# First unit's gate sums between its projections, and the second half's layernorm and gate products among the first three units

## The chip, the cores and the metric

The kernel runs on one core of one Trainium2 chip. The time is the device time of one execution in microseconds (us). The kernel before took 1453.18 us as the median of three runs (1452.86 to 1455.38). One more execution was profiled; all durations and start times in this document come from such profiled executions, counted from the start of the span.

The engines are PE (TensorE, matrix products), DVE (VectorE), ACT (ScalarE), POOL (GpSimd) and SP (SyncE, which here only issues DMAs). Each works off its own queue strictly in the order in which its instructions were written.

## The reference

The input x is 4 sequences of 256 tokens of 256 features, in float32, 1024 tokens in all. The reference has two stages with a residual each:

```
x = x + layernorm(attention(layernorm(x)))
x = x + layernorm(moe(layernorm(x)))
```

The attention is a gated delta net with 16 query/key heads and 32 value heads of width 128. Two projections feed it. One gives q, k, v and z; q, k and v go through a causal convolution over 4 tokens and a silu. The other, with W_ba, gives two numbers per token and value head, b and a, of which the gates are made:

```
beta = sigmoid(b)
g    = -exp(A_log) * softplus(a + dt_bias)
```

g is summed along each chunk of 64 tokens, and differences of the sums, exponentiated, are the decays that weigh the products k k^T and q k^T of a chunk. A triangular system per chunk is solved, and a recurrent state carries from chunk to chunk. The result is normed, gated with silu(z) and projected back with W_out. The second stage routes each token to 6 of 32 experts, beside 2 shared ones.

## The kernel before, in words

The tokens are cut into two halves of 512. A unit is one query/key head on one half, with its two value heads, so there are 32 units: units 0 to 15 on the first half, 16 to 31 on the second. After the units come the experts for both halves.

**The order is written out by hand.** Every stage is a generator that yields places, numbers on one common axis. A heap (L1009 to L1013) always continues the stage with the lowest place, and the instructions that it issues are appended to the queues of PE, ACT, DVE and POOL. So a place decides nothing but the order in the queues. `at(turn, slot)` is turn * 9 + slot; unit u begins at `at(u, 0)` and is spread over about six turns, so several units are in work at any time. `places(p, s)` gives p, p + s, p + 2s and so on. SP's queue is not written by hand: the framework orders the DMAs by itself, from when it thinks that each can go.

**entry(h)** (L207) makes half h ready: it loads x (`load_x`, tile xn), does the layernorm (L188 and L189 statistics on DVE, four times; L190 on DVE and L191, a pow, on POOL; L194 normalises on DVE, four times), transposes it to xT (L204 on PE, L205 copies on ACT), and multiplies with W_ba (L220 on PE, tile pba). Then come the gate sums: the sigmoid to beta (L230, ACT), a + dt_bias (L233, DVE), Abs and Exp (L240, L241, ACT), two sums (L246, L247, DVE), a logarithm (L249, ACT), and reciprocal, products and sums (L250 to L255, DVE). Then the products: cumulative sums of g on PE (L260, L263, tile pc), copied on ACT (L267), negated into ng on DVE (L269, L270), transposed on PE (L278, tile pg), copied on ACT (L279) and stored to DRAM as g_rows (L280). The first group of steps has the places `first`, the products have `second`.

**The stages of a unit.** `weights` loads the projections' weights (L296 w, L303 wz, L307 wo). `decays` loads gw, the unit's rows of g_rows on all partitions (L321), and makes decays of it: POOL adds a mask (L327), and either ACT takes Exp with a bias (unit 0, L338, eight of them) or POOL adds ng (L346) and ACT takes two wide Exps (L350). `prepare` projects q, k and two v (L390, tiles pj_0 to pj_3, PE), convolves (L398 on ACT, three L400 on DVE for each), takes the silu of two at a time (L410, ACT), transposes k and q (L419, ptn_1 and ptn_0) and sums the squares (L421, ACT), makes kk, its reciprocal and br (L427 to L431, DVE) and nk (L435, POOL), multiplies k with k and q (L442 and L461, tiles pk) and weighs the products with the decays (L446 and L464, DVE, tile am). Part of am goes to DRAM as mb (L480). v is transposed and scaled to vp (L490, L493). `blocks`, once for two units, loads small diagonal blocks (L507 wm, L513 on ACT), inverts them on DVE (L514 to L550, tiles quad, dd, prod), stores them (L555 db) and loads them as diag (L563, eight DMAs). `solve` has POOL make e of am (L587), and PE multiplies diag with e (L579, py) and goes on from there. `gate` projects z (L364, pz). `finish` makes the outputs (L664 to L704), transposes them (L736, copied by ACT in L737 to hT) and projects them (L742, pp).

**small** (L772) brings the router's weights and the experts' biases b1 into the chip; b1 is turned by two trips through PE (L791, L800) and DRAM (L794 to L797). It uses the tile `temp`, of which there is one, as do the gate sums. The tile xn, for x, exists once as well.

PSUM tiles under the tag "ms" (pt_a, pba, pc, pg, ptn, pk, ptv, pz) share two banks; the projections pj have two banks of their own. A PE instruction waits until the bank it writes has been read by whoever reads it.

Of the kernel before, what the change touches and what calls it, by code (L numbers as in the profile page):

```python
# [9 lines left out]
AF = mybir.ActivationFunctionType  # L10
# [53 lines left out]
def gated_delta_net_moe(  # L64
# [139 lines left out]
                nc.tensor.transpose(pt[:, i, :], src[:, i, k * P : (k + 1) * P], ident)  # L204
            nc.scalar.copy(xT[:, k, h * T : (h + 1) * T], pt.rearrange("p a b -> p (a b)"))  # L205

    def entry(h, first, second):  # L207

        tl = slice(h * NL, (h + 1) * NL)
        yield next(first)  # L210
        if h:
            load_x("a", h)
        xn = xns[h]
        yield from layernorm(first, xn, xn, 1e-5, f"a_{h}")
        yield from transposed(first, xn, h, f"a_{h}")
        yield next(first)
        pba = bank("ms", [P, NL, HQK, 2, R], f"pba_{h}")
        for t in range(NL):
            for k in range(2):
                nc.tensor.matmul(  # L220
                    pba[:, t].rearrange("p a b c -> p (a b c)"),
                    xT[:, k, h * T + t * P : h * T + (t + 1) * P],
                    wba[:, k, :],
                    start=(k == 0),
                    stop=(k == 1),
                )
        temp = u1.tile([P, 13, NL * HV // 2], F32, tag="temp", name=f"temp_{h}")
        u, sp, w, lw, g = (temp[:, 2 * i : 2 * i + 2, :].rearrange("p a (t h) -> p (a t) h", h=HV) for i in range(5))
        gs = temp[:, 10:13, :].rearrange("p x (b h) -> p b x h", h=HV)
        nc.scalar.activation(  # L230
            beta[:, tl].rearrange("p t (a c) -> p t a c", c=R), pba[:, :, :, 0, :], AF.Sigmoid
        )
        nc.vector.tensor_tensor(  # L233
            u.rearrange("p t (a c) -> p t a c", c=R),
            pba[:, :, :, 1, :],
            dtb.rearrange("p (a c) -> p a c", c=R).unsqueeze(1).to_broadcast([P, NL, HQK, R]),
            ALU.add,
        )
        yield next(first)
        nc.scalar.activation(sp, u, AF.Abs)  # L240
        nc.scalar.activation(sp, sp, AF.Exp, scale=-1.0)  # L241
        if h == 0:
            nc.scalar.activation(alg, alg, AF.Exp)
        yield next(first)

        nc.vector.tensor_scalar(w, sp, 1.0, None, ALU.add)  # L246
        nc.vector.scalar_tensor_tensor(sp, w, 1.0, sp, ALU.subtract, ALU.subtract)  # L247
        yield next(first)
        nc.scalar.activation(lw, w, AF.Ln)  # L249
        nc.vector.reciprocal(w, w)  # L250
        nc.vector.tensor_tensor(sp, sp, w, ALU.mult)
        yield next(first)
        nc.vector.tensor_tensor(sp, lw, sp, ALU.subtract)
        nc.vector.scalar_tensor_tensor(sp, u, 0.0, sp, ALU.max, ALU.add)
        nc.vector.scalar_tensor_tensor(  # L255
            g, sp, -1.0, alg.unsqueeze(1).to_broadcast([P, NL, HV]), ALU.mult, ALU.mult
        )
        yield next(second)
        pc = bank("ms", [P, 3, 2, HV], f"pc_{h}")
        nc.tensor.matmul(  # L260
            pc[:, :2].rearrange("p a b h -> p (a b h)"), inc, g.rearrange("p t h -> p (t h)"), start=True, stop=True
        )
        nc.tensor.matmul(  # L263
            pc[:, 2], ones, g.rearrange("p (b x) h -> p b x h", x=2)[:, :, 0, :], start=True, stop=True
        )
        pcb = pc[:, :2].rearrange("p a b h -> p (a b) h").rearrange("p (b x) h -> p b x h", x=2)
        nc.scalar.copy(gs[:, :, 0:3:2, :], pcb)  # L267
        yield next(second)
        nc.vector.tensor_tensor(gs[:, :, 1, :], pc[:, 2], gs[:, :, 2, :], ALU.add)  # L269
        nc.vector.tensor_scalar(  # L270
            ng[:, tl].rearrange("p (b x) h -> p b x h", x=2), gs[:, :, 0:3:2, :], -1.0, None, ALU.mult
        )
        gr = u1.tile([NE, 2 * 3 * P], F32, tag="gr", name=f"gr_{h}")
        for b in range(2):
            yield next(second)
            pg = bank("ms", [HV, 3, P], f"pg_{h}_{b}")
            for x in range(3):
                nc.tensor.transpose(pg[:, x, :], gs[:, b, x, :], ident)  # L278
            nc.scalar.copy(gr[:HV, b * 3 * P : (b + 1) * 3 * P], pg.rearrange("p a b -> p (a b)"))  # L279
        nc.sync.dma_start(g_rows[:, h * 6 * P : (h + 1) * 6 * P], gr[:HV])  # L280
# [9 lines left out]
    def weights(u):  # L290

        hq = units[u][0]
        c = hq * 6 * P
        yield at(-1, 3)
        w = wp.tile([P, 2, 4 * P], F32, tag="w", name=f"w_{u}")
        nc.sync.dma_start(w, w_qkvz[:, c : c + 4 * P].rearrange("(k p) o -> p k o", p=P))  # L296
        state[u]["w"] = w
        if u == 0:
            nc.sync.dma_start(cw, conv_w)
            nc.sync.dma_start(nw, norm_w)  # L300
        yield at(2, 4)
        w = wp.tile([P, 2, 2 * P], F32, tag="wz", name=f"wz_{u}")
        nc.sync.dma_start(w, w_qkvz[:, c + 4 * P : c + 6 * P].rearrange("(k p) o -> p k o", p=P))  # L303
        state[u]["wz"] = w
        yield at(4, 1)
        w = wp.tile([P, R, D], F32, tag="wo", name=f"wo_{u}")
        nc.sync.dma_start(  # L307
            w, w_out[hq * R * P : (hq + 1) * R * P, :].rearrange("(r p) d -> p r d", p=P)
        )
        state[u]["wo"] = w  # L310
        yield at(4, 5)
        nc.gpsimd.tensor_scalar(w, w, nw, None, ALU.mult)

    def decays(u):

        hq, bp = units[u]
        yield at(-1, 6) if u > 1 else 7.3 - at(u, 0)
        gw = u2.tile([P, R, 2, 3, P], F32, tag="gw", name=f"gw_{u}")
        state[u]["gw"] = gw
        with tc.issue_after(state[u - 2]["wm"].ins) if u > 2 and u % 2 else nullcontext():  # L320
            state[u]["gw_load"] = nc.sync.dma_start(  # L321
                gw.rearrange("p r b x c -> p r (b x c)"),
                g_rows[hq * R : (hq + 1) * R, bp * 6 * P : (bp + 1) * 6 * P].partition_broadcast(P),
            )
        yield at(0, 1.5) if u else 7.5
        gd = gw.rearrange("p r b x c -> p (r b) x c")[:, :, 0:3:2, :]
        nc.gpsimd.tensor_tensor(  # L327
            gd, gd, neg.unsqueeze(1).unsqueeze(1).to_broadcast([P, 2 * R, 2, P]), ALU.add
        )
        if u == 0:  # L330
            for b in range(2):
                for r in range(R):
                    yield 10.4 + 0.4 * b + 0.2 * r
                    h = hq * R + r
                    for x in range(2):
                        t = bp * NL + 2 * b + x
                        y = gw[:, r, b, 2 * x : 2, :] if x == 0 else gw[:, r, b, 2:3, :]
                        nc.scalar.activation(y, y, AF.Exp, bias=ng[:, t, h : h + 1])  # L338
            return

        for x, cols in enumerate((slice(0, 2), slice(2, 3))):
            for r in range(R):
                n = cols.stop - cols.start
                g = ng[:, bp * NL + x : (bp + 1) * NL : 2, hq * R + r]
                y = gw[:, r, :, cols, :].rearrange("p b x c -> p b (x c)")
                nc.gpsimd.tensor_tensor(y, y, g.unsqueeze(2).to_broadcast([P, 2, n * P]), ALU.add)  # L346
        for r in range(R):
            yield at(0, 4.2) + 0.8 * r
            y = gw[:, r].rearrange("p b x c -> p (b x c)")
            nc.scalar.activation(y, y, AF.Exp)  # L350
# [420 lines left out]

    def small():  # L772

        yield at(3, 0)
        full = nh // P
        raw = u1.tile([P, 13, NL * HV // 2], F32, tag="temp", name="b1_raw")
        flat_, turned = raw[:NE, 2:5, :].rearrange("p a b -> p (a b)")[:, :DH], raw[: full + 1, 6:8, :]
        turned = turned.rearrange("p a b -> p (a b)")[:, :P]
        b1f = dram.tile([nh], F32, name="b1f")
        cuts = (slice(0, P), slice(P, DH))  # L780
        with tc.issue_after(state[1]["wm"].ins):
            nc.sync.dma_start(rw, router_w.rearrange("(k p) e -> p k e", p=P))
            nc.sync.dma_start(rb, router_b.partition_broadcast(P))
            nc.sync.dma_start(b2s, b2)
            for i, rows in enumerate(cuts):
                nc.sync.dma_start(raw[: rows.stop - rows.start, i, :NE], b1[rows, :])
        yield at(4, 0.65)
        pb = bank("ms", [NE, DH], "pb1")
        for i, rows in enumerate(cuts):
            n = rows.stop - rows.start  # L790
# [1 line left out]
        nc.scalar.copy(flat_, pb)  # L792
        nc.vector.memset(turned, 0.0)
        nc.sync.dma_start(b1f.rearrange("(e h) -> e h", h=DH), flat_)  # L794
        yield at(4, 0.66)
        nc.sync.dma_start(turned[:full], b1f[: full * P].rearrange("(i p) -> i p", p=P))
        nc.sync.dma_start(turned[full:, : nh - full * P], b1f[full * P :].rearrange("(i p) -> i p", i=1))  # L797
        yield at(5, 0.65)
        pb = bank("ms", [P, full + 1], "pb1t")
        nc.tensor.transpose(pb, turned, ident[: full + 1, : full + 1])  # L800
        nc.scalar.copy(b1s, pb)
# [185 lines left out]
    def begin(place, stage):  # L987
        heapq.heappush(parts, (place + next(stage), len(begun), place, stage))
        begun.append(stage)

    stages = [
        entry(0, places(-9, 0.3), places(6.8, 0.1)),
        entry(1, places(at(6, 0), 1.4), places(at(12, 0), 1.4)),
        small(),
        zeros(),
        post(0, places(at(HQK + 4, 6), 1.4)),
# [66 lines left out]
```

## Time and profile before

| | |
|---|---|
| median of three runs | 1453.18 us (1452.86 to 1455.38) |
| the profiled execution | 1453.36 us |
| its span | 1451.6 us |
| PE busy | 1373.8 us, 95% of the span |
| weight loads of PE busy | 917.4 us, 63% |
| ACT busy | 854.8 us, 59% |
| DVE busy | 833.8 us, 57% |
| POOL busy | 554.0 us, 38% |

The profile's page gives busy times, the span in 40 slices with a digit for the busy tenths of each, and groups of instructions. A timeline lists instructions in order of time: start, duration, engine, source line, operation, output and inputs, count, and in brackets the idle time of the engine just before it and what ended it. For a group of several instructions the duration is that from the first start to the last end. Starts on PE overlap, since matrix products are pipelined. One product in float32 is recorded as two rows, so a projection pj is four. "SPq" is the issue of a DMA, not its transfer. "PEclk" is the share of its full clock that PE was granted.

### The profile page before, as it was taken

To read this page: it belongs to the slowest core of one execution; us is meant where nothing else is said; L and a number is where in the kernel's file an instruction comes from. 1 tells how busy PE (TensorE), PEld (TensorE's weight loads), DVE (VectorE), ACT (ScalarE), POOL (GpSimd) and SP (SyncE) were. 2 spreads that over 40 slices of the span, in tenths; PEclk is the share of its full clock that TensorE was granted. 3 is DMA by queue.
4 is the path that set the end of the run, shared out by engine and by line. 5 is a ranking of instruction groups with operands and counts; after the bars stand their busy time and mean duration, and the time that the engine had idled before them with its cause. 6 is when DMAs were issued, how large, how long until landed. Compare 5 with 4: busy or idle time off the path is not lost.

```text
span 1451.6 us, 29732 instructions
## 1 busy us (share of the span) xinstructions
PE 1373.8 (95%) x11655; PEld 917.4 (63%) x11655; DVE 833.8 (57%) x1726; ACT 854.8 (59%) x2086; POOL 554.0 (38%) x430
## 2 busy tenths in 40 slices
PE   5669999999999999999999999999899999999996
PEld 3336777777777777777777677777765544444443
DVE  4576685867576686758768686766522243232122
ACT  3657768777777777777777777777443222222121
POOL 1354454555454455545544555545511100000000
PEclk9779999999999999999999999999999999999998
DMA  3443433425242442524243342523333565555531
GB/s 117 119 105 90 96 80 93 98 66 128 59 119 70 96 95 65 127 76 105 71 110 72 88 99 74 133 65 81 78 102 91 142 159 140 149 155 149 154 84 35
DMA packets 310156, 146.40 MB, mean 101 GB/s; under 512 B 240780, under 2 KB 281150, under 8 KB 310018
## 3 DMA queue, kind: packets, MB, share of 16 engines
q1 hardware_dynamic: 310018, 144.51, 39.5%
q8 instruction: 93, 1.52, 0.4%
q14 instruction: 45, 0.37, 0.1%
HBM read 129.40 MB, written 15.06 MB: 100 GB/s over the span
## 4 chain that ended last, share of the span: by engine, by line
PE 77%; ACT 11%; DVE 7%; issue 3%; DMA 2%; POOL 1%; POOLq 0%; SPq 0%; ACTq 0%; DVEq 0%
PE ph L915 11%; PE py L935 11%; PE pj L390 9%; PE pz L364 7%; PE pp L742 7%; PE py L579 4%; PE pu L664 4%; PE po L679 4%; PE pd L579 4%; ACT junk L421 3%; DVE c L400 3%; ACT junko L688 3%; PE pk L461 2%; PE pm L711 2%; PE pk L442 2%
## 5 line engine op out<-in xcount | busy, mean ns | idle before, releaser
L400 DVE SCALAR_TENSOR_TENSOR c<-pj,cw,c 128x510 f32<-128x510 f32 (+2 forms) x384 | 286.3, 746 | 153.2 <-ACT c L398 144.1
L702 POOL TENSOR_TENSOR rs<-rs,nhalf 128x4 f32<-128x4 f32 x64 | 66.6, 1040 | 505.0 <-DVE rs L698 295.2
L390 PE MATMUL pj<-xT,w 128*128 128x512 f32 x512 | 247.4, 607 | 4.7 <-DVE c L400 4.6
L918 ACT ACTIVATE h<-ph,b1s 128x512 f32<-128x512 f32 (+1 forms) x94 | 64.6, 687 | 242.6 <-PE ph L915 242.4
L915 PE MATMUL ph<-xT,we 128*128 128x512 f32 (+1 forms) x376 | 177.4, 594 | 2.0 <-ACT phi L615 1.3
L935 PE MATMUL py<-hg,we 128*128 128x512 f32 (+1 forms) x376 | 176.4, 593 | 0.0
L924 DVE TENSOR_TENSOR hg<-h,gb 128x512 f32<-128x512 f32 (+1 forms) x94 | 65.8, 701 | 186.4 <-ACT h L918 180.5
L398 ACT ACTIVATE c<-pj,cw 128x512 f32<-128x512 f32 x128 | 87.4, 685 | 139.3 <-PE pj L390 138.8
L587 POOL TENSOR_TENSOR e<-am,cst 64x1024 f32<-64x1024 f32 x64 | 151.5, 2367 | 2.4
L390 PEld LDWEIGHTS pj<-xT,w 128*128 128x128 f32 x512 | 95.1, 196 | 77.6 <-issue 73.4
L742 PE MATMUL pp<-wo,hT 128*128 128x256 f32 x512 | 126.0, 389 | 7.7 <-ACT hT L737 5.3
L935 PEld LDWEIGHTS py<-hg,we 128*128 128x128 f32 (+1 forms) x376 | 71.3, 190 | 90.5 <-issue 89.1
L742 PEld LDWEIGHTS pp<-wo,hT 128*128 128x128 f32 x512 | 95.8, 192 | 45.4 <-ACT hT L737 31.1
L694 DVE TENSOR_TENSOR hm<-po,sz 128x512 f32<-128x512 f32 x64 | 43.8, 685 | 135.1 <-ACT junko L688 123.2
L364 PE MATMUL pz<-wz,xT 128*128 128x256 f32 x512 | 121.2, 380 | 0.0
L915 PEld LDWEIGHTS ph<-xT,we 128*128 128x128 f32 (+1 forms) x376 | 69.6, 189 | 80.9 <-issue 78.1
L346 POOL TENSOR_TENSOR gw<-gw,ng 128x512 f32<-128x512 f32 (+1 forms) x124 | 99.3, 832 | 2.4
L364 PEld LDWEIGHTS pz<-wz,xT 128*128 128x128 f32 x512 | 92.5, 190 | 10.4 <-issue 0.5
L191 POOL TENSOR_TENSOR rs_d<-rs_d,nhalf 128x2 f32<-128x2 f32 x4 | 2.8, 696 | 248.0 <-DVE rs_d L190 248.0
L446 DVE SCALAR_TENSOR_TENSOR am<-pk,br,gw 128x512 f32<-128x512 f32 x128 | 89.9, 744 | 6.4 <-ACT gw L338 4.5
L442 PE MATMUL pk<-c 128*128 128x512 f32 x128 | 74.3, 663 | 17.3 <-DVE am L446 10.2
L327 POOL TENSOR_TENSOR gw<-gw,cst 128x1024 f32<-128x1024 f32 x32 | 75.4, 2357 | 35.4 <-DMA gw<-g_rows 35.4
(183 smaller groups left out, 2704.1 us busy)
## 6 DMA issues: line engine op xcount, KB each, us to landing
gw<-g_rows SPq DMA_DIRECT2D x32, 768.0 KB, 6.5
w<-in_w_qkvz SPq DMA_DIRECT2D x32, 512.0 KB, 4.0
diag<-db SPq DMA_DIRECT2D x128, 128.0 KB, 3.2
we<-in_w SPq DMA_DIRECT2D x126, 128.0 KB, 2.9
gb<-gate_rows SPq DMA_DIRECT2D x34, 256.0 KB, 3.8
wz<-in_w_qkvz SPq DMA_DIRECT2D x32, 256.0 KB, 2.7
wo<-in_w_out SPq DMA_DIRECT2D x32, 256.0 KB, 2.7
mb<-am SPq DMA_DIRECT2D x64, 128.0 KB, 2.7
```

The lines of the kernel that those rows point to most:

```text
L346: nc.gpsimd.tensor_tensor(y, y, g.unsqueeze(2).to_broadcast([P, 2, n * P]), ALU.add)
L364: nc.tensor.matmul(pz[:, j].rearrange("p r e -> p (r e)"), xT[:, k, t * P : (t + 1) * P], state[u]["wz"][:, k, :], start=(k == 0), stop=(k ...
L390: nc.tensor.matmul(pj.rearrange("p b s -> p (b s)"), state[u]["w"][:, k, col * P : (col + 1) * P], xT[:, k, bp * T : (bp + 1) * T], start= ...
L398: nc.scalar.activation(y, pj, AF.Copy, scale=cw[:, row, 3:4])
L400: nc.vector.scalar_tensor_tensor(y[:, :, back:], pj[:, :, : S - back], cw[:, row, 3 - back : 4 - back], y[:, :, back:], ALU.mult, ALU.add,)
L442: nc.tensor.matmul(pk, s[:, 1, b * S : b * S + P], s[:, 0:2, b * S : (b + 1) * S], start=True, stop=True)
L446: nc.vector.scalar_tensor_tensor(am[:, r, b, 0:4, :].rearrange("p (i x) c -> p i (x c)", i=2), pk, br[:, 2 * b, r : r + 1], gw[:, r, b, 0: ...
L579: nc.tensor.matmul(po[to, h, :], lhsT[g, h, :], rhs[g, h, :], start=True, stop=True)
L587: nc.gpsimd.tensor_tensor(e[g], mt[g, :, g].unsqueeze(1).to_broadcast(full), lev[g].unsqueeze(2).to_broadcast(full), ALU.mult,)
L742: nc.tensor.matmul(pp[:, b, :], hT[:, b, r, :], state[u]["wo"][:, r, :], start=(r == 0), stop=(r == R - 1))
L915: nc.tensor.matmul(ph[:rows], w[:, k * P : k * P + rows], xT[:, k, c], start=(k == 0), stop=(k == 1))
L935: nc.tensor.matmul(py[m], w[:rows, 2 * P + m * P : 2 * P + (m + 1) * P], hgs[i // 3][:rows, i % 3 * T : (i % 3 + 1) * T], start=False, sto ...
```

## The change

The gate sums and the second half's preparation get other places, and two operations move:

- In `entry`, the places are split in three: `first` for layernorm, transposes and the product with W_ba, a new `middle` for the rest of the gate sums, `second` for the products. For the first half, `middle` runs before unit 0's projections as before, and the products go from place 6.8 to 4.65, between its second and third projection. For the second half, `first` starts at 19.0 in steps of 0.6 (turn 2) instead of 54 in steps of 1.4; `middle` starts at 54, and the products stay at 108.
- The Exp of A_log goes to the beginning. The sigmoid is taken last, after the logarithm; until then beta holds a plain copy of b.
- Unit 0's gw is taken at place 4.7 and its mask added at 4.8; the tile of unit 1's wz is taken a turn earlier.
- `small` goes from turns 3 to 5 to turns 14 to 16, behind the last use of `temp` by the second half's gates.

```diff
-    def entry(h, first, second):
+    def entry(h, first, middle, second):
         tl = slice(h * NL, (h + 1) * NL)
         yield next(first)
         if h:
             load_x("a", h)
+        else:
+            nc.scalar.activation(alg, alg, AF.Exp)
...
-        nc.scalar.activation(
-            beta[:, tl].rearrange("p t (a c) -> p t a c", c=R), pba[:, :, :, 0, :], AF.Sigmoid
-        )
+        nc.scalar.copy(beta[:, tl].rearrange("p t (a c) -> p t a c", c=R), pba[:, :, :, 0, :])
...
-        yield next(first)
+        yield next(middle)
         nc.scalar.activation(sp, u, AF.Abs)
         nc.scalar.activation(sp, sp, AF.Exp, scale=-1.0)
-        if h == 0:
-            nc.scalar.activation(alg, alg, AF.Exp)
-        yield next(first)
+        yield next(middle)
         nc.vector.tensor_scalar(w, sp, 1.0, None, ALU.add)
         nc.vector.scalar_tensor_tensor(sp, w, 1.0, sp, ALU.subtract, ALU.subtract)
-        yield next(first)
+        yield next(middle)
         nc.scalar.activation(lw, w, AF.Ln)
         nc.vector.reciprocal(w, w)
         nc.vector.tensor_tensor(sp, sp, w, ALU.mult)
-        yield next(first)
+        nc.scalar.activation(beta[:, tl], beta[:, tl], AF.Sigmoid)
+        yield next(middle)
...
     def weights(u):
-        yield at(2, 4)
+        yield at(2, 4) - (at(1, 0) if u == 1 else 0)
...
     def decays(u):
-        yield at(-1, 6) if u > 1 else 7.3 - at(u, 0)
+        yield at(-1, 6) if u > 1 else (4.7, 7.3 - at(1, 0))[u]
...
-        yield at(0, 1.5) if u else 7.5
+        yield at(0, 1.5) if u else 4.8
...
     def small():
-        yield at(3, 0)
+        yield at(14, 0)
...
-        with tc.issue_after(state[1]["wm"].ins):
+        with tc.issue_after(state[11]["wm"].ins):
...
-        yield at(4, 0.65)
+        yield at(15, 0.65)
...
-        yield at(4, 0.66)
+        yield at(15, 0.66)
...
-        yield at(5, 0.65)
+        yield at(16, 0.65)
...
-        entry(0, places(-9, 0.3), places(6.8, 0.1)),
-        entry(1, places(at(6, 0), 1.4), places(at(12, 0), 1.4)),
+        entry(0, places(-9, 0.3), places(-3, 0.3), places(4.65, 0.01)),
+        entry(1, places(19.0, 0.6), places(at(6, 0), 1.4), places(at(12, 0), 1.4)),
```

What it does to the queues, read from the built program: on PE, pc and pg stand before pj_2 of unit 0; the second half's pt_a_0 stands before pj_3 of unit 2, and pt_a_1 and pba behind it. On DVE, the second half's statistics stand between br, am and L400 of turn 2, the first L194 before L464 of unit 1, the next ones around L400 of pj_2 of unit 2, and L233 among the quads. On POOL, L191 stands behind the e of unit 0. On ACT, Abs and Exp stand before the squares at the beginning of turn 6, and logarithm and sigmoid after the copy of that turn's second projection. On SP, w of unit 2 stands behind gw and db instead of before g_rows, the loads of `small` leave the place before the first db<-dd, and b1f and its two loads stand among eight loads of diag.

## The prediction

> **What bounds the kernel now.** I read the page's slices first.
>
> ```profile
> PE   5669999999999999999999999999899999999996
> ...
> DVE  4576685867576686758768686766522243232122
> ...
> POOL 1354454555454455545544555545511100000000
> PEclk9779999999999999999999999999999999999998
> ```
>
> Each digit is a slice of 36.3 us. From the fourth slice on PE is full and its clock is granted whole; only the first three (5, 6, 6 tenths) hold idle PE. So a change can do two things: move the moment at which PE becomes full, or change PE's work and its short waits after it. I call the first the entry. Then the timelines of the engines, to see what the entry waits for:
>
> ```profile
> 97.56 0.45 PE L579 MATMUL py<-diag,e 64*64 64x64 f32 x2 [5.58 <-DMA diag<-db]
> ```
>
> ```profile
> 35.43 0.35 SPq L280 DMA_DIRECT2D g_rows<-gr  x1
> 37.28 0.89 SPq L321 DMA_DIRECT2D gw<-g_rows  x2
> ...
> 90.02 1.29 SPq L555 DMA_DIRECT2D db<-dd  x2
> 93.14 6.03 SPq L563 DMA_DIRECT2D diag<-db  x8
> ```
>
> ```profile
> 68.28 0.16 DVE L427 TENSOR_SCALAR kk<-ss 128x4 f32<-128x4 f32 x1
> ...
> 73.92 1.65 DVE L464 SCALAR_TENSOR_TENSOR am<-pk,br,gw 128x256 f32<-128x256 f32 x4
> 76.54 2.31 DVE L400 SCALAR_TENSOR_TENSOR c<-pj,cw,c 128x510 f32<-128x510 f32 x3 [0.97 <-ACT c L398]
> 79.31 2.31 DVE L400 SCALAR_TENSOR_TENSOR c<-pj,cw,c 128x510 f32<-128x510 f32 x3 [0.45 <-ACT c L398]
> ...
> 83.47 0.15 DVE L523 TENSOR_TENSOR quad<-dd 128x8 f32<-128x8 f32 x1 [1.77 <-issue]
> ```
>
> The entry is at 97.56: PE's first solve product waits 5.58 us for diag, which follows db<-dd at 90.02, which follows DVE's chain from quad at 83.47. Before that DVE and ACT take turns, and the whole row hangs on gw, loaded after g_rows at 35.43. I call "shift" how much later (plus) or earlier (minus) an instruction stands than in the row of before.
>
> **Step 1, gate sums (L230 to L255), start of the span.** The sigmoid goes behind the logarithm, the Exp of alg goes to the front (its input must be in by 10.37, when ACT first copies). Gone from the path are the load at L241 (16.11 to 17.40, 1.29) and alg's place in the queue (17.62 to 17.85, 0.23): DVE's first L400 moves from 21.66 to 20.14, -1.52. The sigmoid's load and itself (1.28 + 0.28) now stand after Ln on ACT, 17.84 to 19.4; the copy of the first projection follows (0.59, to 20.0) just under DVE's 20.14, so the cover is 0.14 and whatever ACT is later than that goes onto the path. The row has the Exp 1.29 after the start of its load, with nothing between. [...]
>
> **Step 2, the products between projections two and three.** Six L400 end at 24.66. The silu's load and silu (26.25 to 28.61 before) end at 27.07, the copy of pc (0.26) at 27.33; from L269 to the store took 1.77 (33.66 to 35.43), so g_rows goes out at 29.1, shift -6.3. w_2 no longer stands before it on SP: its load waits until pj_3 of unit 0 is done (33.9) and is wanted at 54.5, so it is covered. gw lands 8.3 after the store (35.43 to 43.69) at 37.4, POOL's L327 (2.35) ends at 39.8.
>
> The price: pj_2 and pj_3 of unit 0 stand behind pg on PE, so they start at 28.56 instead of 24.11. From 24.11 to the copy of pj_3 took 5.36 at half clock, so that copy is at 33.9, DVE's two triples (2.22 each) end at 37.25 (33.74 before), the silu's end starts the squares at 38.26 and the next projection's copy at 39.7. Then the Exp's load (1.29) and eight Exps (46.13 to 48.91, 2.78): c pj_1 of unit 1 starts at 44.35, 48.91 before. pk_2 and am follow at -4.4, and the mb store of unit 0 goes from 54.88 to 50.5. **Shift after the first unit -4.4.** It could be -6.3, all of g_rows' lead, or -3.2, what the first am pair has (43.4 against 46.67); I take the value of ACT's queue, since it releases what follows.
>
> **Step 3, the second half's layernorm in turn 2.** kk of unit 1 is at 63.9. DVE now carries four bn pairs among am and L400 (about 0.53 each): the last ends at 71.6. Next on DVE stands the first of four normalisations (L194), waiting for POOL's pow (L191), and behind it L464 of unit 1, L400 of pj_2 and pj_3, qe, the quads. POOL's queue has the pow behind e:
>
> ```profile
> 68.52 1.02 POOL L435 TENSOR_TENSOR nk<-kk,half 128x4 f32<-128x4 f32 x1 [15.86 <-DVE kk L427]
> 69.51 2.35 POOL L327 TENSOR_TENSOR gw<-gw,cst 128x1024 f32<-128x1024 f32 x1
> 71.94 3.19 POOL L346 TENSOR_TENSOR gw<-gw,ng 128x512 f32<-128x512 f32 x4
> 75.08 4.81 POOL L587 TENSOR_TENSOR e<-am,cst 64x1024 f32<-64x1024 f32 x2
> ```
>
> nk starts with kk, so at shift -4.4 e ends at 75.5 and the pow (1.04) at 76.55: DVE stands still 4.9. Then L194 (0.34), L464 (1.55) to 78.5, L194, L400, two L194, to 81.8. On PE the transposes pt_a_0 stand before pj_3 of unit 2 and need all four normalisations: pj_3 starts at 81.95 instead of running ahead. PE was nearly idle from 72.6, and its clock will be at half:
>
> ```profile
> 72.39 3.29 PE L390 MATMUL pj<-xT,w 128*128 128x512 f32 x4
> ...
> 76.39 1.88 PE L390 MATMUL pj<-xT,w 128*128 128x512 f32 x4
> ```
>
> The first of these rows is a projection at half clock (next start 3.13 later), the second one at full clock (1.72). I take 3.13, the row after a like idle; the other end is 1.4 less. The copy is at 85.25, DVE's triple runs 85.95 to 88.2 (79.31 to 81.5 before). pt_a_1 and its copy (0.58) end at 86.45, pba takes 1.9 (1.74 + 0.17 in its row at 230.51; 3.25 in the first, at 11.86: the upper end is 1.4 more), its copy ends at 88.65, and L233, put between the quads, takes 0.29. The second quad stands at 89.0 against 83.85: **entry shift +5.15**. In terms: -4.4, bn 2.2, POOL wait 4.9, normalisations 1.4, wait for pj_3 4.15, L233 0.1, minus DVE's own waits in that stretch that vanish (0.97 + 0.45 + 1.77 = 3.2). Ends: +1.9 (shift -6.3, full clock) and +7.8 (shift -3.2, slow pba).
>
> **Step 4, work taken out of the full stretch.** Turn 7 loses the transposes (0.53 at 220.08, 0.44 at 226.56) and pba (1.74): -2.7 of PE.
>
> **Step 5, waits in the full stretch.** Between 200 and 280 PE waited 0.32, 0.81 (behind a bn on DVE), 1.72 (for hT, behind the loads at L241 and L410) and 1.14 (for the squares): 4.0, of which 3.4 go; stretches without this work have 0.1 to 0.2 in 40 us. Now Abs, load and Exp (1.83) stand before the squares of turn 6:
>
> ```profile
> 180.45 0.58 ACT L737 COPY hT<-pth 128x512 f32<-128x512 f32 x1
> ```
>
> pp starts on PE at 181.09, when that copy has just ended (181.03): +1.6. Load, Ln, load, sigmoid (3.1) stand before the squares of ptn_0: pk_2 waits 1.0 more, so 2.6 in all. Net -0.8; ends -3.4 (all hidden) and +1.5 (the full 4.9 felt).
>
> **Step 6, the b1 preparation, turns 3 to 5 to turns 14 to 16.** PE, ACT and DVE pieces cost the same there. SP gets the store b1f and two loads among the eight diag loads. The fourth diag load stands at +1.3 (three issues at 0.45 each, the landing of b1f, 1.5, mostly under two diag issues); in the steady rows it lands at 480.0 for a product at 480.55: +0.8, ends 0 and 2. The five small loads leave SP at 81.87 to 84.1, where it was idle. xn_b moves ahead of db<-dd, ready when pt_a_1 is done (86), 9 us before db<-dd at 95.2. The places of gw and wz change no order on POOL, and wz_1 was issued at 5.69 already: 0.
>
> **Sum.** +5.15 - 2.7 - 0.8 + 0.8 = +2.45. The profiled execution took 1453.36 (span 1451.6 and 1.76 around it); it becomes 1455.8. The median of the runs is 0.18 lower: **1455.6**.
>
> **Rivals.**
> - Slower still: the burst of table loads in turn 6 is felt in full (+1.5 for -0.8), b1f holds diag for 2 and pba runs at 3.25. 2.45 + 2.3 + 1.2 + 1.4 = +7.3, 1460.5. For it: ACT had no slack at 180.45. Against it: the squares of ptn_0 release only pk_2.
> - Faster: DVE does not stand behind e. Place: POOL's queue in turn 2; price 4.9, and 1.4 more as PE then keeps its clock: 2.45 - 6.3 = -3.9, 1449.3. It decides once the wait for the pow with what follows falls by 5.4. Against it: e runs directly behind L346 in the row of before, and the pow is queued behind it.
> - The loss is given back: the turn 6 loads and b1f hide under PE's own work; 5.15 - 2.7 - 3.4 = -0.95, 1452.2. For it: ACT is idle 3.8 us before its next projection copy at 184.84. Against it: PE is in order and has hardly any slack to take from.
>
> **How the numbers follow.** What this kernel's runs can tell from no change is about 0.2%, 2.9 us. My forecast has 0.45, with its own range 1453.6 to 1457.8, of which some two fifths lies beyond 2.9; slower still 0.27; faster 0.13; given back 0.15. So slower 0.19 + 0.27 = 0.46, same 0.26 + 0.15 = 0.41, faster 0.13. The range leaves out most of the faster case and the top of the slowest: 1450.3 to 1461.0.
>
> **What would show it.** g_rows' store near 29 and the first mb store near 50.5 (steps 1, 2); a DVE wait of about 5 us on POOL before L194 near 71 to 76, with e just before the pow (step 3); py at about 102.7 for 97.56; PE waits near turn 6 and none around 250 (step 5); one late diag near turn 15 (step 6). The forecast is wrong if DVE's wait is short, if the entry is not near +5, or if the later PE waits are not within 2 us of those named.

## The result, and the profile after

The changed kernel took 1461.56 us (median of 7 runs, 1457.51 to 1463.65); the kernel before, in the same comparison, 1455.42 (7 runs, 1452.86 to 1458.23). The ratio is 1.0036, with a 95% interval of 1.002 to 1.0052: 5.2 us slower. (The two medians alone lie 6.1 apart; this document goes by the ratios throughout.) The profiled execution took 1461.47, its span is 1459.6 against 1451.6.

The page's slices:

```profile
PE   5759989999999999999999999999899999999997
...
DVE  4666767768576676868777586767522143131222
...
POOL 1433545456554545655554455545421100000000
PEclk9879999999999999999999999999999999999998
```

PE has more to do in the second slice (7 for 6) and less in the third and the sixth (5 for 6, 8 for 9): the third slice, 73 to 109 us, holds the later entry, the sixth, 182 to 219, turn 6. SP's timeline, the issues of the DMAs:

```profile
29.39 0.35 SPq L279 DMA_DIRECT2D g_rows<-gr  x1
31.21 0.89 SPq L321 DMA_DIRECT2D gw<-g_rows  x2
...
50.26 1.36 SPq L480 DMA_DIRECT2D mb<-am  x2
...
95.14 1.35 SPq L555 DMA_DIRECT2D db<-dd  x2
98.21 6.07 SPq L563 DMA_DIRECT2D diag<-db  x8
```

g_rows goes out 6.04 earlier (35.43 before), mb of unit 0 4.62 earlier (54.88), db<-dd 5.12 later (90.02). What lies between the last two is POOL's and DVE's turn 2, here from the timelines of these engines:

```profile
67.05 3.19 POOL L346 TENSOR_TENSOR gw<-gw,ng 128x512 f32<-128x512 f32 x4
70.20 4.77 POOL L587 TENSOR_TENSOR e<-am,cst 64x1024 f32<-64x1024 f32 x2
75.05 1.02 POOL L191 TENSOR_TENSOR rs_a<-rs_a,nhalf 128x4 f32<-128x4 f32 x1
```

```profile
71.04 1.53 DVE L190 TENSOR_SCALAR rs_a<-mv_a 128x4 f32<-128x4 f32 x1
76.11 0.41 DVE L194 TENSOR_SCALAR xn_a<-xn_a,mv_a,rs_a 128x256 f32<-128x256 f32 x1 [3.53 <-POOL rs_a L191]
76.43 1.66 DVE L464 SCALAR_TENSOR_TENSOR am<-pk,br,gw 128x256 f32<-128x256 f32 x4
...
85.98 2.31 DVE L400 SCALAR_TENSOR_TENSOR c<-pj,cw,c 128x510 f32<-128x510 f32 x3 [4.71 <-ACT c L398]
...
88.97 0.16 DVE L523 TENSOR_TENSOR quad<-dd 128x8 f32<-128x8 f32 x1
```

The pow stands behind e, and DVE behind the pow: from 71.04, when the sum L190 could start, to 76.11 there is no other work on DVE. Then it stands 4.71 for the copy of pj_3, which PE could not begin before all four normalisations. On PE, ptv_1 of unit 1 stands ahead of both the transposes and pj_3, and waits for L464, which is behind the pow too:

```profile
78.14 1.11 PE L490 MATMUL ptv<-cst,c 128*128 128x128 f32 x4 [5.63 <-DVE am L464]
79.05 0.63 PE L204 MATMUL pt_a<-cst,xn_a 128*128 128x128 f32 x2
81.00 0.80 PE L204 MATMUL pt_a<-cst,xn_a 128*128 128x128 f32 x2 [1.32 <-DVE xn_a L194]
81.59 3.62 PE L390 MATMUL pj<-xT,w 128*128 128x512 f32 x4
```

The entry, on PE's timeline:

```profile
102.55 0.44 PE L579 MATMUL py<-diag,e 64*64 64x64 f32 x2 [6.02 <-DMA diag<-db]
```

It is 4.99 later than before. Had the rest gone as predicted, the kernel would have gained 2.7 after it; it lost 3 instead. Where, is best seen in the shift of one mark per turn, the first product of pz_0 (L364), which stands in turn u + 3 for unit u. Each number is the start in the kernel's own PE timeline minus that of before (107.86, 134.25, 167.86, 199.96, 235.30, 269.65 for units 0 to 5). Unit 3's mark lies behind the beginning of turn 6, where the gate sums now are; "again" is a second profile of the changed kernel, and the others are the experiments below.

| kernel | unit 0 | 1 | 2 | 3 | 4 | 5 | 11 | 15 |
|---|---|---|---|---|---|---|---|---|
| changed | 6.38 | 5.93 | 9.02 | 13.51 | 11.30 | 8.51 | 8.53 | 9.05 |
| changed, again | 5.33 | 4.88 | 5.07 | 8.94 | 6.23 | 3.43 | 3.42 | 3.70 |
| first unit's part alone | -4.83 | -4.82 | -5.75 | -5.76 | -5.76 | -4.12 | -4.13 | -4.12 |
| second half's part alone | 10.44 | 9.99 | 10.37 | 14.23 | 11.49 | 8.70 | 8.70 | 8.98 |
| pow before e | 3.19 | 4.12 | 4.83 | 11.06 | 8.45 | 5.65 | 5.65 | 5.94 |
| transposes behind pj_3 | 7.09 | 8.01 | 10.30 | 14.19 | 11.52 | 8.73 | 8.72 | 9.00 |
| late gate sums | 8.42 | 7.97 | 11.50 | 10.96 | 7.17 | 7.17 | 8.57 | 8.85 |
| normalisations early | -3.34 | -3.80 | -3.20 | 0.66 | -2.10 | -4.90 | -4.93 | -4.66 |
| layernorm in gaps | -1.31 | -1.77 | 1.18 | 0.63 | -3.15 | -3.15 | -2.05 | -1.77 |
| all in gaps | 0.54 | 0.09 | -0.77 | -1.31 | -5.10 | -7.89 | -7.90 | -7.62 |
| all in gaps, tight | -3.59 | -2.69 | -1.58 | -2.13 | -5.91 | -8.71 | -8.73 | -8.47 |

The changed kernel loses at the entry, in turn 5 (unit 1 to 2, +3.09) and in turn 6 (unit 2 to 3, +4.49), and gains 5.0 in turns 7 and 8. Turn 6 on PE's timeline:

```profile
191.75 3.57 PE L742 MATMUL pp<-wo,hT 128*128 128x256 f32 x8 [1.75 <-ACT hT L737]
...
202.51 1.13 PE L461 MATMUL pk<-c 128*128 128x256 f32 x4 [2.20 <-ACT junk L421]
```

The eight products of pp take 3.57 where 1.99 is usual. The busy times in stretches of 2 us (PE, PEld, DVE, ACT, POOL, then PE's granted clock, the DMA share and GB/s) tell why: the clock fell to half just as pp began.

```profile
190.00:192.00 2.00, 0.25 (x1) 0.26 (x2) 0.75 (x1) 1.66 (x6) 0.00 (x0) 0.89 0.00 0
192.00:194.00 2.00, 2.00 (x5) 1.58 (x6) 1.86 (x6) 0.00 (x0) 0.29 (x1) 0.50 0.00 0
194.00:196.00 2.00, 2.00 (x6) 1.28 (x5) 1.91 (x6) 0.00 (x0) 1.92 (x3) 0.76 0.00 0
```

### The profile page after: what moved, and what is told of

Same layout as the page of the kernel before. It is cut to its first block, busy times and chain, and to the rows that moved or that the text cites. A ratio compares the mean times of both kernels' runs of the same rounds, so it can differ in the third digit from the quotient of the medians.

```text
span 1459.6 us, 29731 instructions
## 1 busy us (share of the span) xinstructions
PE 1376.9 (94%) x11655; PEld 919.6 (63%) x11655; DVE 837.1 (57%) x1726; ACT 853.9 (59%) x2086; POOL 553.8 (38%) x430
## 3 DMA queue, kind: packets, MB, share of 16 engines
q8 instruction: 93, 1.52, 0.4%
## 4 chain that ended last, share of the span: by engine, by line
PE 77%; ACT 10%; DVE 7%; DMA 3%; issue 2%; POOL 1%; SPq 0%; POOLq 0%; ACTq 0%; DVEq 0%
PE ph L915 11%; PE py L935 11%; PE pj L390 10%; PE pz L364 7%; PE pp L742 7%; PE py L579 4%; PE pu L664 4%; PE po L679 4%; PE pd L579 4%; ACT junk L421 3%; DVE c L400 3%; ACT junko L688 2%; PE pm L711 2%; PE pk L461 2%; PE pk L442 2%
## 5 line engine op out<-in xcount | busy, mean ns | idle before, releaser
L400 DVE SCALAR_TENSOR_TENSOR c<-pj,cw,c 128x510 f32<-128x510 f32 (+2 forms) x384 | 286.2, 746 | 157.0 <-ACT c L398 147.9
L364 PE MATMUL pz<-wz,xT 128*128 128x256 f32 x512 | 121.2, 380 | 0.0
L346 POOL TENSOR_TENSOR gw<-gw,ng 128x512 f32<-128x512 f32 (+1 forms) x124 | 99.3, 832 | 2.4
L364 PEld LDWEIGHTS pz<-wz,xT 128*128 128x128 f32 x512 | 92.5, 190 | 10.4 <-issue 0.5
L191 POOL TENSOR_TENSOR rs_d<-rs_d,nhalf 128x2 f32<-128x2 f32 x4 | 2.8, 696 | 248.0 <-DVE rs_d L190 248.0
L688 ACT ACTIVATE junko<-po 128x128 f32<-128x128 f32 x256 | 71.1, 278 | 29.2 <-PE po L683 12.0
```

Of the source, the lines that this page charges most:

```text
L364: nc.tensor.matmul(pz[:, j].rearrange("p r e -> p (r e)"), xT[:, k, t * P : (t + 1) * P], state[u]["wz"][:, k, :], start=(k == 0), stop=(k ...
L400: nc.vector.scalar_tensor_tensor(y[:, :, back:], pj[:, :, : S - back], cw[:, row, 3 - back : 4 - back], y[:, :, back:], ALU.mult, ALU.add,)
L688: nc.scalar.activation(junk, po[:, b, r, :], AF.Square, accum_out=os_[:, x, b, r : r + 1])
```

## The experiments

My theory was: the first unit's part is a gain of 4.4, the second half's layernorm costs 9.5 in the ramp because DVE stands behind POOL's queue and PE behind DVE, and the table loads of turn 6 give back part of what turns 7 and 8 gain. The rivals were that the two parts do not add, that the ramp's loss has another cause than the queues, and that turn 6 lost its time otherwise than by the gate sums.

**First unit's part alone.** `first` of the second half, its gate sums and `small` stand where they were.

```diff
-        entry(1, places(19.0, 0.6), places(at(6, 0), 1.4), places(at(12, 0), 1.4)),
+        entry(1, places(at(6, 0), 1.4), places(at(6, 0) + 16.8, 1.4), places(at(12, 0), 1.4)),
...
-        yield at(14, 0)
+        yield at(3, 0)
```

> The first unit's part alone: the gate sums and products between its second and third projection, sigmoid last; the second half's layernorm, gate sums and the b1 preparation where the kernel before has them. Theory (the first unit's part is a gain of 4.4 at the entry, and the loss is all the second half's): py's first product at 93.2 instead of 97.56, time 1451.0, ratio 0.9970 (0.996 to 0.998). Rival (an earlier entry is swallowed by later waits in turns 3 to 8, for diag and on ACT, as the changed kernel lost 3.1 in turn 5): py at 93.2 but ratio 0.9985 or more.

Measured: 1449.41, ratio 0.9966 (0.9952 to 0.9979). PE's timeline (this kernel's lines lie six further down, L585 is L579):

```profile
92.80 0.45 PE L585 MATMUL py<-diag,e 64*64 64x64 f32 x2 [5.50 <-DMA diag<-db]
```

The entry is 4.76 earlier, and nearly all of it is kept. The theory holds; the rival falls.

**Second half's part alone.** The first unit as in the kernel before, everything else as in the changed one.

```diff
-        entry(0, places(-9, 0.3), places(-3, 0.3), places(4.65, 0.01)),
+        entry(0, places(-9, 0.3), places(-9 + 3.6, 0.3), places(6.8, 0.1)),
```

> The second half's part alone: its layernorm in turn 2, its gate sums in turn 6 with the sigmoid last, the b1 preparation in turns 14 to 16; the first unit as in the kernel before. Theory (the two parts add): py's first product at 97.56 + 4.99 + 4.4 = 106.95, time 1455.4 + 5.2 + 4.4 = 1465, ratio 1.0066 (1.005 to 1.008). Rival (without the lead of the first unit the pow's wait hides under waits that DVE and PE have in the ramp anyway): py at 104 or earlier, ratio 1.0045 or less.

Measured: 1463.12, ratio 1.0069 (1.0052 to 1.0085). Here too L585 is L579.

```profile
107.24 0.45 PE L585 MATMUL py<-diag,e 64*64 64x64 f32 x2 [6.08 <-DMA diag<-db]
```

The entry is 9.68 later than before; -4.76 and +9.68 make 4.92, against 4.99 in the changed kernel. The parts add, at the entry and in the ratios (-0.0034 and +0.0069 against +0.0036).

**Pow before e.** The fourth bn pair and, with it, L190 and the pow have in the changed kernel the same place as e, 21.4, and e goes first. Here they have 21.39.

```diff
-        entry(1, places(19.0, 0.6), ...
+        entry(1, itertools.chain((19.0, 19.6, 20.2, 20.8, 21.39), places(22.001, 0.6)), ...
```

> The changed kernel, with the fourth bn pair of the second half's layernorm one hundredth of a slot earlier (place 21.39 for 21.40), so that its pow (L191) stands in POOL's queue just before e of unit 0 instead of just behind it; on DVE the fourth bn pair and L190 come before the am pair of pk_1 instead of after it; nothing else moves. Theory (POOL's queue makes DVE stand): the stand of DVE before the first L194 falls from about 4.9 us to 1.0 to 1.5, py's first product comes at 98 to 99 instead of 102.55, the time falls by about 4, to 1457.5, ratio to the kernel before 1.0010 (1.000 to 1.002). e ends about 1 to 2 us later, which nobody waits for. Rival (the layernorm's own DVE work and pt_a_0 standing before pj_3 set the entry, and the wait for the pow only took time in which DVE would have stood anyway): py at 101.5 or later, time within 1 of the changed kernel, ratio 1.003 or more.

Measured: 1458.53, ratio 1.0026 (1.0012 to 1.0041), py at 99.88: 2.7 to 3.1 earlier than in the two profiles of the changed kernel (102.55 and 102.96), not 4. POOL and DVE:

```profile
70.32 1.02 POOL L191 TENSOR_TENSOR rs_a<-rs_a,nhalf 128x4 f32<-128x4 f32 x1
71.31 4.77 POOL L587 TENSOR_TENSOR e<-am,cst 64x1024 f32<-64x1024 f32 x2
```

```profile
71.48 2.33 DVE L194 TENSOR_SCALAR xn_a<-xn_a,mv_a,rs_a 128x256 f32<-128x256 f32 x1
73.72 1.65 DVE L464 SCALAR_TENSOR_TENSOR am<-pk,br,gw 128x256 f32<-128x256 f32 x4
75.29 0.95 DVE L194 TENSOR_SCALAR xn_a<-xn_a,mv_a,rs_a 128x256 f32<-128x256 f32 x1
...
83.50 2.31 DVE L400 SCALAR_TENSOR_TENSOR c<-pj,cw,c 128x510 f32<-128x510 f32 x3 [4.40 <-ACT c L398]
```

The wait is gone, but the first L194 lasts 2.33 instead of 0.41: it ends at 73.81, just after the first of e's two instructions (the second starts at 73.73). So it ran beside e and took 1.92 longer there. And DVE's stand for pj_3 is still 4.40. Both theories miss in size; what is left after the pow is the other stand.

**Transposes behind pj_3.** To price that stand, pt_a_0 and pt_a_1 go behind pj_3 of unit 2, and pba behind the quads; the pow stays behind e.

```diff
-        entry(1, places(19.0, 0.6), ...
+        entry(1, itertools.chain(itertools.islice(places(19.0, 0.6), 9), (24.75, 25.0, 28.0)), ...
```

> The changed kernel, with pt_a_0 and pt_a_1 of the second half behind pj_3 of unit 2 in PE's queue instead of before it, and pba behind them, after the last quad products; the layernorm with its wait for the pow stays. In the run with the pow first the wait of DVE for pj_3's copy stayed at 4.40 us and the entry came only 2.7 earlier than in the changed kernel. Theory (the two DVE terms of the ramp stand in series: about 2.5 to 3 for the pow behind e, about 4 for pj_3 behind the transposes): DVE's last L400 of unit 2 no longer waits, py's first product at 98.2 to 99.5 instead of 102.55, ratio to the kernel before 1.0008 (1.000 to 1.002). Rival (pj_3 would be late anyway, as PE is at half clock there and the last L194 waits for the pow): py at 101 or later, ratio 1.0025 or more.

Measured: 1460.74, ratio 1.004 (1.0028 to 1.0052), py at 104.22. DVE's wait for pj_3's copy fell from 4.71 to 2.15, and yet nothing came earlier. PE, ACT and SP show what took its place:

```profile
78.22 1.12 PE L490 MATMUL ptv<-cst,c 128*128 128x128 f32 x4 [5.54 <-DVE am L464]
79.12 3.61 PE L390 MATMUL pj<-xT,w 128*128 128x512 f32 x4
```

```profile
89.54 0.42 ACT L513 ACTIVATE dd<-wm 128x256 f32<-128x256 f32 x1 [5.11 <-DMA wm<-mb]
```

```profile
82.77 0.38 SPq L295 DMA_DIRECT2D w<-in_w_qkvz  x1
83.64 0.37 SPq L108 DMA_DIRECT2D xn_b<-in_x  x1
84.19 0.37 SPq L507 DMA_DIRECT2D wm<-mb  x1
```

First, pj_3 stands behind ptv_1 of unit 1, which waits for a PSUM bank that L464 must read first, and L464 is behind the first L194 and so behind the pow: DVE's stand reaches pj_3 by another way. Second, SP's order, which nobody wrote, came out differently: wm stands behind w, which waits for pj_3, and behind xn_b, which waits for pt_a_1. In the changed kernel wm goes out at 81.47, before both. The theory falls for this edit, and the rival has the number but not the whole reason. What the stand for pj_3 costs at the entry was not priced by it. It does show how pj_3's lateness is made up: pj_3 starts at 79.12 instead of 81.59, so about 2.5 of it are the transposes', and the rest is ptv_1's wait, which the changed kernel has as well (5.63).

**Late gate sums.** The layernorm stays in turn 2, the sums go back to turns 7 and 8.

```diff
-        entry(1, places(19.0, 0.6), places(at(6, 0), 1.4), places(at(12, 0), 1.4)),
+        entry(1, places(19.0, 0.6), places(at(6, 0) + 16.8, 1.4), places(at(12, 0), 1.4)),
```

> The changed kernel, with the second half's gate sums (Abs, Exp, Ln, sigmoid and the DVE steps between) at the places of the kernel before, in turns 7 and 8, instead of the first part of turn 6. The layernorm stays in turn 2. Theory (the burst of table loads ahead of hT and the squares is what cost 4.5 in turn 6): the 1.75 and 2.20 us waits of PE in 190 to 205 are gone and PE's granted clock there stays at 1.00; the waits of turns 7 and 8 return, 2 to 3 of the 5 gained there; net 1.5 to 2.5 less than the changed kernel, ratio 1.0022 (1.0015 to 1.0027). Rival (the sums cost the same wherever they stand, and turn 6 lost its time otherwise): within 0.7 of the changed kernel, ratio 1.0032 to 1.0041.

Measured: 1457.61, ratio 1.0026 (1.0015 to 1.0037), about 1.5 less than the changed kernel; the two intervals overlap, so the times alone do not show the difference, and the profiles have to. The waits of turn 6 are gone (-0.54 there in the table), those of turns 7 and 8 are back, 1.72 and 1.15. From unit 2 to unit 11 this kernel goes from 11.50 to 8.57, -2.9; the changed one, again, from 5.07 to 3.42, -1.65. So the sums cost 1.3 more in turn 6 than where they were. The sign is the theory's, the size its lower end. This profile lost 3.5 in turn 5, without any gate sums near, so turn 5 has nothing to do with them.

**The changed kernel again**, unedited, to see what of the first profile repeats.

> The changed kernel itself, unedited, once more. Theory (which waits are followed by half clock is chance, the waits themselves are not): the same waits within 0.3 us at the same instructions of PE (hT 1.75, junk 2.20 in turn 6), but half-clock slices after other ones of them than in the first profile; ratio 1.0036 again (1.002 to 1.005). Rival (the half clock belongs to the order of the work): half-clock slices at the same places, after the hT wait of turn 6 and at py of turn 5.

Measured: 1460.30, ratio 1.0036 (1.0022 to 1.005) once more. The profiled execution has a span of 1453.7, 5.9 less than the first; with 1455.56 us it is the fastest of the twelve executions of this run. PE in turn 6, and the stretches around the same wait:

```profile
187.78 1.99 PE L742 MATMUL pp<-wo,hT 128*128 128x256 f32 x8 [1.74 <-ACT hT L737]
...
193.00 1.12 PE L442 MATMUL pk<-c 128*128 128x512 f32 x2 [0.41 <-DVE am L446]
196.97 1.13 PE L461 MATMUL pk<-c 128*128 128x256 f32 x4 [1.30 <-ACT junk L421]
```

```profile
186.00:188.00 2.00, 0.26 (x2) 0.22 (x2) 0.71 (x1) 1.70 (x6) 0.00 (x0) 1.00 0.00 0
188.00:190.00 2.00, 2.00 (x9) 1.60 (x9) 1.86 (x7) 0.00 (x0) 0.25 (x1) 1.00 0.00 0
```

The wait for hT is the same to 0.01, and the clock does not fall. In turn 5 PE waited 0.60 for diag, not 0.95 and 0.63, and the clock stayed whole there too. What repeats is the row "again": +5.33 at the entry, +3.87 in turn 6, -5.51 in turns 7 and 8. The theory holds; two of its details do not: the wait of 2.20 was not the same again, but 0.41 and 1.30, with 0.75 for L464 behind them (at 205.80).

**Normalisations early.** Only the bn pairs, the pow and the L194 leave turn 2, for stretches in which DVE is idle; the transposes and pba stay among the projections, the sums in turn 6.

```diff
-        entry(1, places(19.0, 0.6), ...
+        entry(1, iter((8.8, 9.0, 9.1, 9.2, 9.3, 16.4, 16.5, 16.6, 16.7, 24.41, 25.0, 25.6)), ...
```

> The changed kernel, with only the second half's bn pairs, pow and normalisations moved out of turn 2 into DVE's idle stretches before the first projections of units 1 and 2; pt_a_0 stays before pj_3 of unit 2, pt_a_1 and pba behind it, and the gate sums in turn 6. Theory (the loss in the ramp is DVE's stand and the transposes' wait for the normalisations, and not the transposes and pba themselves): pj_3 no longer waits, py's first product at 93.5 to 95.5 instead of 102.5 to 103.0; turn 6 keeps its waits of 1.74, 0.4 and 1.3; ratio to the kernel before 0.9970 (0.9955 to 0.9985). Rival (pt_a_0, pt_a_1 and pba at half clock among the projections cost 3 or more themselves): py at 97 or later, ratio 0.999 or more.

Measured: 1451.92, ratio 0.9983 (0.9969 to 0.9996).

```profile
94.21 0.44 PE L579 MATMUL py<-diag,e 64*64 64x64 f32 x2 [6.21 <-POOL gw L346]
```

The theory holds. (The row names POOL's L346, which ended just then; what py needs of POOL is e, which was done at 74.59. The eight loads of diag were issued from 89.98 on, so the wait is taken to be for diag, as in the other kernels.) This prices what the run with the transposes could not. Between this kernel and the changed one lie 8.34 (to 102.55) and 8.75 (to 102.96): DVE's work, its stand and what PE waited for behind it. Between this kernel and the first unit's part alone lie 1.41: the transposes and pba themselves. Together 9.75, which is the whole cost of the second half's part at the entry. Turn 6 costs the same again, +3.86.

**Layernorm in gaps.** As before, and the transposes and pba go into PE's wait of 5.5 us ahead of py; the sums are in turns 7 and 8.

```diff
-        entry(1, places(19.0, 0.6), places(at(6, 0), 1.4), places(at(12, 0), 1.4)),
+        entry(1, iter((8.8, 9.0, 9.1, 9.2, 9.3, 16.4, 16.5, 16.6, 16.7, 30.5, 30.6, 30.65)),
+              places(at(6, 0) + 16.8, 1.4), places(at(12, 0), 1.4)),
```

> The changed kernel, with the second half's layernorm in idle stretches that the profile of the first unit's part alone shows: the four bn pairs in DVE's 3.2 us before the first projection of unit 1 (37.6 to 40.8), the four L194 in its 4.4 us before the first projection of unit 2 (57.2 to 61.7), the transposes and pba in PE's 5.5 us before py (87.3 to 92.8); the gate sums in turns 7 and 8 as in the kernel before. Theory (the layernorm costs nothing in the ramp once nothing critical is queued behind it, and takes 2.7 us of PE work and a 0.8 us wait out of turn 7): py at 93.2 to 94, time 1447, ratio 0.995 (0.9935 to 0.9965). Rival (the ramp's chain of units is pushed by every instruction put into it): py at 95 or later, ratio 0.9965 or more, no better than the first unit's part alone.

Measured: 1449.50, ratio 0.9963 (0.9947 to 0.9979), as good as the first unit's part alone and no better. The ratio is at the upper end of the theory's range, and py is as late as the rival said, but not for its reason. The layernorm is free now: db<-dd goes out at 85.46, against 85.34 there. But the gap ahead of py does not hold the transposes and pba:

```profile
90.17 1.12 PE L204 MATMUL pt_a<-cst,xn_a 128*128 128x128 f32 x4 [2.77 <-DVE am L446]
91.97 1.11 PE L204 MATMUL pt_a<-cst,xn_a 128*128 128x128 f32 x4 [0.68 <-ACT xT L205]
93.76 3.68 PE L222 MATMUL pba<-wba,xT 128*128 128x64 f32 x16 [0.68 <-ACT xT L205]
97.36 1.97 PE L579 MATMUL py<-diag,e 64*64 64x64 f32 x32
```

They wait for banks and for copies, pba takes 3.68 where 1.90 stands in the kernel before (at 230.51), and py begins at 97.36; in the first unit's part alone, with db<-dd at the same time, it began at 92.80. These 4.6 eat up what turns 6 to 8 give (1.18 to -3.15 in the table).

**All in gaps.** The transposes go behind pk_1 of unit 1, pba behind pj_3 of unit 2, and the sums into idle stretches of ACT in the ramp.

```diff
-        entry(1, places(19.0, 0.6), places(at(6, 0), 1.4), places(at(12, 0), 1.4)),
+        entry(1, iter((8.8, 9.0, 9.1, 9.2, 9.3, 16.4, 16.5, 16.6, 16.7, 21.5, 21.55, 24.75)),
+              iter((25.37, 27.5, 29.85, 30.45)), places(at(12, 0), 1.4)),
```

> As the run before it, with the transposes after pk_1 of unit 1, pba after pj_3 of unit 2, and the gate sums in ACT's and DVE's idle stretches of the ramp too (Abs and Exp right behind the copy of wm, where the Exp table is already loaded; Ln and sigmoid in ACT's 7 us before the silu at 92.3). Theory (the waits of turns 7 and 8, 1.7 and 1.1 us, go too): py at 93.2 to 94.5, no PE wait over 0.9 us between 180 and 290, time 1444.5, ratio 0.9935 (0.992 to 0.9955). Rival (the sums push the quads and the silu in the ramp by 1 to 3 us): py at 95 to 97, ratio 0.996 or more.

Measured: 1446.47, ratio 0.9937 (0.9919 to 0.9955). No PE wait over 0.31 is left between 142 and 290. py stands at 96.45, as the rival said, since pk_2 of unit 1 starts 3.6 later behind the transposes; the time is the theory's all the same, as turns 6 to 8 now give 7.1.

**All in gaps, tight.** The transposes go behind pj_3 of unit 2, just before pba, and the load of xn_b is held behind wm, in front of which it would stand here as in the run with the transposes.

```diff
-16.7, 21.5, 21.55, 24.75)),
+16.7, 24.71, 24.72, 24.75)),
...
-        load_x("b", h)
+        with nullcontext() if h else tc.issue_after(state[1]["wm"].ins):
+            load_x("b", h)
```

> The run with everything in idle stretches, with pt_a_0 and pt_a_1 behind pj_3 of unit 2 and just before pba, instead of before pk_2 of unit 1, where they held pk_2 for 3.6 us and DVE for 2.3; and the load of xn_b behind wm on SP, as wm would stand behind it there. Theory (py comes at 93 to 94, as in the first unit's part alone, with the waits of turns 6 to 8 gone): time 1443, ratio 0.9920 (0.990 to 0.9935). Rival (pba and the copies of pt_a hold the copy of wm and the quads by 1 to 3 us): py at 94.5 to 96.5, ratio 0.9932 or more.

Measured: 1443.67, ratio 0.9921 (0.9907 to 0.9935): 11.6 less than the kernel before, 1455.25 in this comparison.

```profile
92.14 0.45 PE L579 MATMUL py<-diag,e 64*64 64x64 f32 x2 [5.12 <-DMA diag<-db]
```

It has the early entry of the first unit's part (92.80) and the lighter turns 6 to 8. The same work that cost 9.7 at the entry where the change put it costs nothing at the entry here. It is not free behind it: at unit 2 this kernel stands at -1.58 and the first unit's part alone at -5.75. Between py and that mark lie a wait for diag of 0.53 right behind py, half clock from 119.45 to 122.86 (behind the 1.80 that PE waits for the squares), 1.25 for y instead of 0.70, and 0.28 and 0.86 for diag in turn 5.

## Why the prediction was right or wrong

The forecast was +2.45; measured are +5.2, with an interval from +2.9 to +7.6. Set on the median of 1453.18 that the forecast started from, the ratio gives 1458.4, against the 1455.6 forecast. The direction and the mechanism were right, the size was too small.

- **Step 1 (gate sums, -1.52) and step 2 (products, -4.4)** were right. DVE's first L400 stands at 20.19 for the predicted 20.14, g_rows at 29.39 for 29.1, mb at 50.26 for 50.5, and the part alone moves the entry by -4.76. In turn 6 of the changed kernel ACT's next instruction starts 1.29 to 1.30 after the start of each load (185.84 to 187.14, 197.78 to 199.07, 199.40 to 200.69), as the prediction's 1.29 has it; the time that the forecast missed is made up otherwise, as said below.
- **Step 3 (second half's layernorm, entry +5.15)** was right in sum and cause: 4.99 and, again, 5.40; alone, +9.68 for the 9.55 that the terms give without the -4.4. The stand for the pow lies between 71.04 and 76.11, as predicted. What I got wrong inside it is the meaning of the term "POOL wait 4.9", which I priced in the faster rival as 4.9 plus 1.4 to be had by freeing DVE from e. Freed, it gave 2.7 to 3.1, as L194 then ran beside e and took 2.33. This rival would not have been faster by its own place alone. The prediction also let pj_3 wait for the normalisations only; ptv_1, which stands ahead of it and waits 5.63 for L464, holds PE until 79.05 of the 81.59.
- **Step 4 and the removed waits of step 5 (-2.7 and -3.4)** came to -5.51 for -6.1: of the waits named all are gone, and two small new ones have come (0.76 for y, 0.31 for hT). With the sums out of turn 6 as well, turns 6 to 8 give 7.1.
- **The added waits of step 5 (+2.6 in turn 6)** are the term that was mis-sized: +3.87 in every profile with a whole clock there (3.86 to 3.89 in the three profiles of other edits that have it too). hT was right (1.74 for 1.6). pk_2 was 1.30 for 1.0, and behind it came a wait that the prediction did not have, 0.75 of ptv_1 for L464, which stands on DVE behind the late pk_2.
- **Step 6 (b1, +0.8)** came to nothing. The row "again" rises by 0.28 there (unit 11 to unit 15, 3.42 to 3.70), but PE has no wait between 455 and 540 us, so the late diag load was covered. The rise comes with b1's own two products on PE (473.76 to 474.18), which stood in turn 4 before.
- **Not in the prediction**: half clock inside the full stretch. In the first profile it makes the greater part of the 5.4 between the row "changed" and the row "changed, again" at unit 15; the rest is a turn 5 in which PE waited 1.58 for diag, not 0.60. Without it the row "again" ends at +3.70, 1.25 above the forecast: +1.3 in turn 6 and +0.6 in turns 7 and 8, less 0.5 for b1 and 0.1 elsewhere. At the end this profile's span is only 2.1 above that of before: 1.8 come back between the units and the experts, by a wait for diag that is 0.8 shorter there (1.86 for 2.64) and by half clock of 3.41 us (from 1052.83) where the kernel before had 6.83 (from 1048.02; the changed kernel's first profile has 3.41 too, from 1058.55). On the other hand this is the fastest of twelve executions, and the median of these is 4.7 higher. The mean granted clock of each execution says why in the main: it is 0.982 in the three fastest (1455.56 to 1456.89 us) and 0.978 in four of the slower ones (1460.30 to 1462.28). Which waits are followed by half clock in those no profile shows, so how the measured 5.2 is shared between waits and half clock stays open.

Of the rivals, "the loss is given back" is excluded by turn 6. "Slower still" had the burst of turn 6 right in direction, but b1f, which it also needed, cost less and not more.

## What to carry to other kernels

Before work is put into an idle stretch, ask of each instruction what it waits for and what stands behind it in its queue: the layernorm cost 9.7 us in a ramp with idle time on every engine, and did not move the entry once its pow, its normalisations and its transposes each stood where nothing critical was queued behind them. After a move, look again at the queues that nobody wrote by hand, here SP's, and at the rotating PSUM banks, since both carried the old wait to a new place in the run with the transposes behind pj_3 (5.11 for the copy of wm, 5.54 for ptv_1). And keep PE's waits short: here a wait of 1.7 us for hT cost 1.7 in seven profiles and, with half clock behind it, 3.0 to 3.4 in three.

## What was not expected of the hardware

**The clock fell after some short waits and not after others like them.** Between 117 and 290 us, the two kernels, the changed one's second profile and the nine edits show 27 PE waits of 1.59 to 1.84 us. After 6 of them the granted clock is at 0.50 in one of the next 2 us stretches, after 21 it stays at 1.00. They are the same waits: the 1.8 of pk_1 for the squares, in turn 4, is in all twelve profiles, and half clock follows it in three. The wait for hT is followed by it in 3 of 10. Two waits for diag close together (0.41 and 0.87) were followed by half clock in one profile (layernorm in gaps, 0.50 from 155.45 to 157.45), while after 0.69 and 1.05 the clock stayed at 1.00 in another (transposes behind pj_3). With half clock behind the wait for hT, pp takes 1.3 to 1.7 more (3.26 to 3.64 for 1.99). Each of these stretches of half clock lasts 3.4 us (191.56 to 194.97 in the first profile), and in the traces of the kernel before and of the changed one all changes of the granted clock lie whole multiples of 3.41 us apart. Why the same wait of 1.8 is followed by half clock in three profiles and not in nine was not shown.

**Two DVE instructions lasted longer beside POOL's e, and the profile shows them as long, not as waiting.** In the run with the pow before e, the first L194 takes 2.33 beside e, from 71.48, and ends with e's first instruction; in the changed kernel it takes 0.41 behind e. L190, on 128x4 elements, takes 0.17 before and 1.53 in the changed kernel (71.04 to 72.57), where e's first instruction runs from 70.20 for 2.36 on average. Not every instruction beside e was longer: with the pow before e, L464 took its usual 1.65 beside e's second instruction (73.72), and in the changed kernel L188, the statistics on xn_a, its usual 0.42 beside e's first (70.37). L190 and L194 read and write SBUF, as L188 does, and L464 reads pk, in PSUM. What sets the two apart was not shown, as no run was made for this alone.
